# Softmax row sums in a four-layer fp32 kernel: fewer partial sums, two residual buffers, pinned order

## The chip, the cores and the metric

The kernel runs on one core of one Trainium2 chip. The metric is the time of one execution on the device in microseconds (us), taken as the median of several runs. Five engines work side by side, each through its own queue of instructions: TensorE (PE, matmuls; PEld is its weight load), VectorE (DVE), ScalarE (ACT), GpSimd (POOL) and SyncE (SP). DMAs are started from the queues of SP, ACT and POOL.

## The reference

Four layers, each added to its own normalised input, over a tensor of 4 x 384 x 64 x 64 in fp32. Only the first layer is touched:

```python
x_attn = x[:, :PD]            # PD = 96 of 384 channels
x_skip = x[:, PD:]
...
q = qkv[:, :QK].reshape(B, QK, N)          # QK = 16, N = 4096
k = qkv[:, QK:2 * QK].reshape(B, QK, N)
v = qkv[:, 2 * QK:].reshape(B, VD, N)
attn = jax.nn.softmax(jnp.einsum('bcn,bcm->bnm', q, k) * scale, axis=-1)
out = jnp.einsum('bcn,bmn->bcm', v, attn).reshape(B, VD, H, W)
xm = jax.nn.relu(jnp.concatenate([out, x_skip], axis=1))
y = jnp.einsum('oc,bchw->bohw', w_proj, xm)
...
x = x + _L0_conv_ref(_gn(x), ...)
```

So each batch needs a 4096 x 4096 softmax attention over 96 value channels, a ReLU, a 384 x 384 projection and the residual sum. Layers 1 to 3 (a local Fourier filter, a gated convolution block, a dynamic 7 x 7 convolution) follow.

## The kernel before

`attention` (L819) runs for batches b = 0 to 3. A batch is eight **blocks** i of 512 queries, and a block is eight **steps** c of 512 keys. One step does this:

- `scores` (L825): four matmuls, one for each group of 32 rows of the array, write the score tile `sc_s` (four PSUM banks, one buffer). ScalarE turns it into two tiles `probs` of 128 x 1024 by `Exp` (L842): `lo` (tag p0, two buffers) and `hi` (tag p1, three buffers). The scores of step c+1 are traced before the products of step c.
- `products` (L850): twelve matmuls of 32 columns, four side by side, add the step into two PSUM banks `av`. Their order on TensorE is fixed by `together` and `issue_after` (L623, L868).
- `add_up` (L871): the softmax denominators. VectorE adds every `lo` into `acc_lo` (L878; none in step 0). GpSimd starts a DMA which copies (steps 0 and 1, L884) or adds (steps 2 to 6, L886) `hi` into one of two accumulators `acc_hi`, even steps into one and odd ones into the other. The last `hi` is used as it is.

At the end of a block `evacuate` (L888) empties `av`: ScalarE copies two pieces of 32 rows to `av_t` (L893, L895), VectorE one piece of 96 rows to `xm` (L894) and one of 32 to `av_t` (L896). `invert` (L899) sums the four partial tiles (last `hi`, odd, `acc_lo`, even) over their partitions with a matmul of ones, 32 matmuls of 128 columns into `sum_m`, and VectorE takes the reciprocal (L919). In step 1 of the next block `finish` (L922) spreads it (`rd_m`, L926), adds the two halves of the block (L933) and applies ReLU and the scale (L934).

`layer0_end` (L962) then loads the residual block `x_res` (L966, 768 KB over SP's queue, pool `blk`, tag xr, one buffer), makes the 288 other rows of `xm` by ReLU on ScalarE (L967, L971), projects (L978), adds into `x_res` (L985), takes statistics (L649) and stores it with a DMA of GpSimd (L988).

Beside batch b runs `others` (L587): statistics and q, k, v of batch b+1 (L687, L701 to L761) and, from b = 1 on, layer 1 of batch b-1 (L1060 to L1177), spread over the 64 steps by `side_by_side` (L600). A scheduler puts each engine's instructions in order from the traced order, priorities and expected times; an engine runs its list strictly in that order. `keep_in_program_order`, which only the new code uses, queues an instruction behind the one traced just before it on the same engine.

After the attention, `late_block` (L1181) gives layer 2 its input blocks: by turns from the pool `blk` and from a pool `late` opened for it (L574). The branch with `maxima` (L777) is inside an `If` which these data don't take.

Of the kernel before, what the change touches and what calls it, by code (L numbers as in the profile page):

```python
# [29 lines left out]
NJ = 3  # L30
# [252 lines left out]
class _Builder:  # L283
# [222 lines left out]
    def phase_a(self, strips):  # L506
# [3 lines left out]
        with ExitStack() as ctx:  # L510
            self.open_psum(ctx, 2)
            self.ln_exp()
            cp = ctx.enter_context(tc.tile_pool(name="a_const", bufs=1))
            pool = lambda name, bufs: ctx.enter_context(tc.tile_pool(name=name, bufs=bufs))
            self.blk = pool("a_blk", 4)
            self.work = pool("a_work", 2)
            attention = ctx.enter_context(ExitStack())
            self.big = attention.enter_context(tc.tile_pool(name="a_big", bufs=1, side="right"))
            self.probs = attention.enter_context(tc.tile_pool(name="a_probs", bufs=2, side="right"))
            for k in ("r0", "m0", "n0"):  # L520
                setattr(self, k, cp.tile([P, NJ, B], F32, tag=k, name=k))
# [12 lines left out]
            self.first_norm(self.x0_st)  # L534
            self.score_shifts(cp)
            self.ln_exp()
            self.w_proj = self.weight(cp, "w_proj_t")
            self.w_in = self.weight(cp, "w_in_t")
            self.w_out = self.weight(cp, "w_out_t")
            q, k4, vt = self.qkv_tiles()  # L540
            for _ in self.qkv(0, q, k4, vt, self.x0):
                pass
            for _ in self.x_norm(0, self.x0_st):
                pass
            w = lambda tag, name: self.work.tile([P, C], F32, tag=tag, name=name)
            pick, fft = w("tt", "pick")[0:40, 0:P], w("cf", "fft")[0:40]
            lo, hi = _CONST_COLS["pick"]
            nc.sync.dma_start(pick, self.ins["consts"][0:40, lo:hi])
            nc.scalar.dma_start(fft, self.ins["fft_t"])
            pf = self.pm("filter_p")  # L550
            nc.tensor.matmul(pf[:, 0:C], lhsT=pick, rhs=fft, start=True, stop=True)
            self.filt = cp.tile([P, C], F32, tag="filt", name="filt")
            nc.vector.tensor_copy(self.filt, pf[:, 0:C])

            a, c = self.bn_scale_shift(
                "bn2", self.vec("bn2_m"), self.vec("bn2_v"), self.vec("bn2_g"), self.vec("bn2_b")
            )
            self.bn2_c = cp.tile([P, NJ], F32, tag="bn2_c", name="bn2_c")
            nc.vector.tensor_copy(self.bn2_c, c)
            m = self.pm("bn2_rows")  # L560
            t = w("tt", "bn2_a").rearrange("p (j n) -> p j n", j=NJ)
            nc.vector.tensor_copy(t, a.unsqueeze(2).to_broadcast([P, NJ, P]))
            for j in range(NJ):
                nc.tensor.matmul(m[:, j * P : (j + 1) * P], lhsT=t[:, j], rhs=self.ident, start=True, stop=True)
            for j in range(NJ):
                nc.vector.tensor_mul(self.w_proj[:, j], self.w_proj[:, j], m[:, 0:C])
            for b in range(B):
                nxt = self.qkv_tiles() if b + 1 < B else None
                self.side_by_side(b, self.attention(b, q, k4, vt), self.others(b, nxt))
                if nxt is not None:  # L570
                    q, k4, vt = nxt

            attention.close()
            self.late = pool("a_late", 1)  # L574
            self.open_strips(strips)
            layer1, done = self.layer1(B - 1), iter(())
            self.last_x1, ahead, left = [None] * 8, [], 4 * (B - 1)
            for n, _ in enumerate(layer1):
                if n == 20:
                    done = self.strips_of(0, range(B - 1))  # L580
                if next(done, True) is None:
                    left -= 1
                elif not left and len(ahead) < 2 and self.last_x1[3 * len(ahead) + 2] is not None:
                    ahead.append(self.ahead_strips(len(ahead)))
            self.last_strips(ahead)
# [43 lines left out]
                last = job()  # L629
        return last  # L630

    def acc_lo(self, name):
        return self.probs.tile([P, 1024], F32, tag="acc_lo", name=name, bufs=1)

    def acc_hi(self, name):
        return self.probs.tile([P, 1024], F32, tag="acc_hi", name=name, bufs=2)

    def norm_of_stats(self, st):
        mv = self.sm([P, NJ, 2], "gn_mv")
# [137 lines left out]
    def maxima(self, b):  # L777
        nc = self.nc
        for _ in self.x_norm(b):
            pass  # L780
        k = [self.probs.tile([P, 1024], F32, tag=f"p{h}", name="mx_k", bufs=2 + h) for _ in range(2) for h in range(2)]
        q = [self.acc_lo("mx_q"), *(self.acc_hi("mx_q") for _ in range(2))]
        q.append(self.probs.tile([P, 1024], F32, tag="p1", name="mx_q", bufs=3))
        q = [t[:, v * 512 : v * 512 + 512] for t in q for v in range(2)]
        for i in range(8):
            xa = self.layer_norm(self.centered(b, i))
            m = self.pm("mx_q_m")
# [31 lines left out]
    def attention(self, b, q, k4, vt):  # L819
# [3 lines left out]
        tc, nc = self.tc, self.nc  # L823

        def scores(i, c):  # L825
            p = [self.probs.tile([P, 1024], F32, tag=f"p{h}", name="probs", bufs=2 + h) for h in range(2)]
            s = self.p4("sc_s")

            with tc.high_priority(3000) if b else nullcontext():
# [41 lines left out]
        def add_up(c, p):  # L871

            lo, hi = p
            if c == 0:
                self.sums = [self.acc_lo("acc_lo")]
                self.lo_first = lo
            else:
                nc.vector.tensor_add(self.sums[0], self.lo_first, lo)  # L878
                self.lo_first = self.sums[0]
            if c == 7:  # L880
                self.sums.append(hi)
            elif c < 2:
                self.sums.append(self.acc_hi("acc_hi"))
                nc.gpsimd.dma_start(self.sums[1 + c], hi)  # L884
            else:
                nc.gpsimd.dma_start(self.sums[1 + c % 2], hi, accum_op=ALU.add)  # L886

        def evacuate(av):  # L888

            xm = self.work.tile([P, NJ, 512], F32, tag="xm", name="xm", bufs=1)  # L890
            t = self.wk("av_t", "rd", 1)
            with tc.high_priority():
                nc.scalar.copy(t[0:32], av[0][96:128])  # L893
                nc.vector.tensor_copy(xm[0:PD, 0], av[0][0:PD])  # L894
                nc.scalar.copy(t[32:64], av[1][0:32])  # L895
                nc.vector.tensor_copy(t[64:96], av[1][32:64])  # L896
            return xm, t

        def invert(sums):  # L899

            m = self.pm("sum_m")
            lo, even, odd, last = sums
            parts = [t[:, v * 512 : v * 512 + 512] for t in (last, odd, lo, even) for v in range(2)]
            jobs = (
                partial(
                    nc.tensor.matmul,
# [15 lines left out]
        def finish(xm, t, rd):  # L922

            m = self.pm("rd_m")
            for g in range(4):
# [4 lines left out]
                    start=True,  # L930
                    stop=True,
                )
            nc.vector.tensor_add(t[0:PD], t[0:PD], xm[0:PD, 0])  # L933
            nc.vector.scalar_tensor_tensor(xm[0:PD, 0], t[0:PD], 0.0, m[0:PD], ALU.max, ALU.mult)  # L934
            return xm

        self.last_av = None
# [4 lines left out]
        for n_step, (i, c) in enumerate(steps):  # L942
# [7 lines left out]
            if c == 7:  # L950
                evacuated = *evacuate(av), invert(self.sums)
            next(end, None)
            if c == 1 and done is not None:
                end = self.layer0_end(b, i - 1, finish(*done), st)
            if c == 7:
                done = evacuated
            yield
# [4 lines left out]
    def layer0_end(self, b, i, xm, st):  # L962

        nc = self.nc
        blk = slice(i * 512, (i + 1) * 512)
        x = self.block("x_res", self.ins["x"][b], i, "xr", 1)  # L966
        nc.scalar.activation(  # L967
            xm[PD:P, 0], x[PD:P, 0], AF.Relu, bias=self.n0[PD:P, 0, b : b + 1], scale=self.r0[PD:P, 0, b : b + 1]
        )
# [208 lines left out]
        if b == B - 1:  # L1178
            self.last_x1[h] = x

    def late_block(self, n):  # L1181
        return (self.late if n % 2 else self.blk).tile([P, NJ, 512], F32, tag="xr", name="in_x1", bufs=1)

    def ahead_strips(self, n):

        x = self.late_block(n)
        self.nc.gpsimd.dma_start(x, self.x1[B - 1][:, 0, n * 1536 : n * 1536 + 1536].rearrange("p (j n) -> p j n", j=NJ))
        return x

# [185 lines left out]
    def strips_of(self, j, batches):  # L1375

        for b in batches:
            for q in range(4):
                x = self.late_block(b * 4 + q)
                self.strips5(j, b, x.rearrange("p j n -> p (j n)")[:, 0:1024], q * 8, self.pa)  # L1380
                yield

# [984 lines left out]
```

## Time and profile before

| what | us |
|---|---|
| median of 3 runs | 4717.23 (4715.02 to 4718.2) |
| the profiled execution, and its span | 4721.59, 4719.6 |
| TensorE busy in the span | 4310.8 (91%) |
| VectorE, ScalarE, GpSimd busy | 2914.9, 2012.4, 983.4 |

The stages, by stretches of the span (busy us of each engine in the stretch):

| stretch | what runs | PE | DVE | ACT |
|---|---|---|---|---|
| 110 to 560 | attention of batch 0, with q, k, v of batch 1 | 399.1 of 450 | 203.6 | 178.9 |
| 560 to 1130 | batch 1, with layer 1 of batch 0 | 533.1 of 570 | 375.5 | 247.9 |
| 1130 to 1690 | batch 2, with layer 1 of batch 1 | 522.5 of 560 | 363.8 | 247.5 |
| 1690 to 2240 | batch 3, with layer 1 of batch 2 | 501.7 of 550 | 341.2 | 221.4 |
| 2240 to 4720 | layer 1 of batch 3, layers 2 and 3 | 2283.1 of 2480 | 1561.6 | 1073.5 |

To read it: a stretch in which TensorE is busy for nearly all of the time is bound by it, and what is left is the sum of its waits. A fp32 matmul shows as two instructions (twice the count of the code). Durations of matmuls are modelled and overlap, so lengths are best taken from start to start.

### The profile page before, as it was taken

The page shows a single profiled execution, that of the slowest core. Times are in us where ns is not written, and L with a number is a line of the kernel's source. Part 1 is how long each engine was busy: PE and PEld are TensorE (multiplying, and loading weights), DVE is VectorE, ACT ScalarE, POOL GpSimd, SP SyncE. Part 2 cuts the span into 40 slices and gives each one's busy share as a digit, 9 for nine tenths or more (in the row PEclk, how much of TensorE's full clock was granted, in tenths as well). Part 3 has the DMA queues.
Part 4 walks back from the last instruction along what each step waited for, and adds up shares of the span by engine and source line. Part 5 has one row for each costly group of instructions (what it writes and reads, how often), then busy time and mean ns, then how long its engine had stood idle before and what let it go on. Part 6 is the DMA issues. An engine that isn't in the chain of part 4 may idle for free. (4 is left out here: it accounts for less than half of the span.)

```text
span 4719.6 us, 60890 instructions
## 1 busy us (share of the span) xinstructions
PE 4310.8 (91%) x23693; PEld 2332.9 (49%) x23693; DVE 2914.9 (62%) x4800; ACT 2012.4 (43%) x2961; POOL 983.4 (21%) x1007
## 2 busy tenths in 40 slices
PE   6899899999999999997998899699999999898998
PEld 2233333334333333332546888644444444498988
DVE  6533576665666756666687788755541112777898
ACT  4344344344444444443644666521114333664342
POOL 1111111110111110110004566300000000145765
PEclk9999999999999999998999999899999999998999
DMA  5644534343344433443325999976666333897897
GB/s 169 163 116 100 145 94 123 105 122 93 103 111 113 118 101 105 112 114 98 112 99 167 333 326 334 313 261 251 249 233 243 123 132 115 302 337 257 249 310 239
DMA packets 316622, 848.52 MB, mean 180 GB/s; under 512 B 25915, under 2 KB 126374, under 8 KB 305062
## 3 DMA queue, kind: packets, MB, share of 16 engines
q1 hardware_dynamic: 213096, 407.56, 27.3%
q0 software_dynamic: 71136, 291.41, 21.3%
q10 hardware_dynamic: 32094, 145.57, 7.8%
q8 instruction: 190, 3.11, 0.3%
q14 instruction: 106, 0.87, 0.1%
HBM read 433.13 MB, written 293.86 MB: 154 GB/s over the span
## 5 line engine op out<-in xcount | busy, mean ns | idle before, releaser
L629 PE MATMUL av<-probs,vt 128*32 128x512 f32 x5632 | 733.7, 611 | 0.0
L842 ACT ACTIVATE probs<-sc_s 128x1024 f32<-128x1024 f32 x512 | 498.5, 1020 | 520.6 <-PE av L629 322.8
L1147 DVE SCALAR_TENSOR_TENSOR acc<-band,vecs,acc 128x512 f32<-128x512 f32 x708 | 498.9, 746 | 45.1 <-POOL band L1106 34.4
L1437 PE MATMUL conv_m<-toep,z 128*128 128x192 f32 (+1 forms) x2304 | 447.4, 352 | 22.3 <-DVE z L1366 12.3
L1804 PE MATMUL h_m<-f_h,cm_w_t 128*128 128x512 f32 x1008 | 436.1, 595 | 7.4 <-ACT f_h L1741 7.4
L1437 PEld LDWEIGHTS conv_m<-toep,z 128*128 128x128 f32 x2304 | 403.1, 195 | 46.4 <-ACT d_o L1448 13.9
L2199 PE MATMUL conv_m<-toep,z 128*128 128x128 f32 x3072 | 377.6, 280 | 22.1 <-DVE toep L2186 9.4
L878 DVE TENSOR_TENSOR acc_lo<-acc_lo,probs 128x1024 f32<-128x1024 f32 x192 | 234.2, 1220 | 232.4 <-ACT probs L842 232.0
L2199 PEld LDWEIGHTS conv_m<-toep,z 128*128 128x128 f32 x3072 | 363.8, 196 | 25.1 <-issue 8.7
L626 PE MATMUL sc_s<-q,k 32*128 32x512 f32 x512 | 297.6, 662 | 76.5 <-ACT probs L842 76.5
L1683 PE MATMUL h_s<-e_tok,cm_w_t 128*128 128x512 f32 x768 | 362.8, 595 | 4.1 <-DVE e_tok L1668 4.1
L629 PEld LDWEIGHTS av<-probs,vt 128*32 128x32 f32 x5632 | 175.6, 112 | 324.8 <-issue 317.6
L886 POOL DMA_DIRECT2D acc_hi<-probs x160 | 137.2, 857 | 909.7 <-ACT probs L842 833.2
L1418 POOL TENSOR_TENSOR toep<-w,band 128x1280 f32<-128x1280 f32 x96 | 278.3, 2899 | 199.3 <-PE conv_m L1437 187.5
L1804 PEld LDWEIGHTS h_m<-f_h,cm_w_t 128*128 128x128 f32 x1008 | 192.5, 191 | 250.6 <-issue 239.7
L629 PE MATMUL sc_s<-q,k 32*128 32x512 f32 x1536 | 301.1, 662 | 0.0
L1068 PE MATMUL t_m<-w_in_t,xb 128*128 128x384 f32 x768 | 292.6, 513 | 6.5 <-DVE coef L1085 4.8
L626 PE MATMUL av<-probs,vt 128*32 128x512 f32 x512 | 281.1, 632 | 10.5 <-DVE av_t L896 7.2
L978 PE MATMUL proj_m<-xm,w_proj_t 128*128 128x512 f32 x576 | 275.3, 614 | 6.8 <-DVE x_res L985 3.7
L1690 ACT COPY e_h<-h_s 128x1024 f32<-128x1024 f32 x96 | 97.2, 1012 | 400.3 <-PE h_s L1683 400.3
L1692 DVE BATCH_NORM_STATS2 h_st<-e_h 128x6 f32<-128x512 f32 x192 | 123.5, 685 | 217.5 <-ACT e_h L1690 217.5
L1683 PEld LDWEIGHTS h_s<-e_tok,cm_w_t 128*128 128x128 f32 x768 | 146.5, 191 | 188.3 <-issue 183.6
(468 smaller groups left out, 6908.4 us busy)
## 6 DMA issues: line engine op xcount, KB each, us to landing
acc_hi<-probs POOLq DMA_DIRECT2D x224, 512.0 KB, 4.5
d<-d_o ACTq DMA_DIRECT2D x48, 1024.0 KB
c_d<-d SPq DMA_DIRECT2D x48, 1024.0 KB
hid<-e_h ACTq DMA_DIRECT2D x16, 3072.0 KB
f_h<-hid SPq DMA_DIRECT2D x14, 3072.0 KB
x_in<-in_x SPq DMA_DIRECT2D x96, 256.0 KB
x_res<-in_x SPq DMA_DIRECT2D x32, 768.0 KB
xa<-x_res POOLq DMA_DIRECT2D x32, 768.0 KB, 3.9
```

The lines of the kernel that those rows point to most:

```text
L626: first = first()
L629: last = job()
L842: nc.scalar.activation(p[h], s[:, 2 * h : 2 * h + 2].rearrange("p a b -> p (a b)"), AF.Exp, scale=0.25,)
L878: nc.vector.tensor_add(self.sums[0], self.lo_first, lo)
L978: nc.tensor.matmul(m, lhsT=self.w_proj[:, j, o * P : (o + 1) * P], rhs=xm[:, j], start=j == 0, stop=j == NJ - 1,)
L1068: nc.tensor.matmul(m[:, 0:C], lhsT=xb[:, j], rhs=self.w_in[:, j, :], start=j == 0, stop=j == NJ - 1,)
L1147: nc.vector.scalar_tensor_tensor(out, src(j, k), w, done, ALU.mult, ALU.add)
L1418: eng.tensor_tensor(t, self.w53[:, at : at + 160].rearrange("p (m n) -> p m n", n=8).unsqueeze(2).to_broadcast([P, 20, 8, 8]), band.rearra ...
L1437: nc.tensor.matmul(m[:, c * 256 + to : c * 256 + to + 64 * (k1 - k0)], lhsT=self.z_[:, at : at + P], rhs=t[:, 10 * c + k0 : 10 * c + k1].r ...
L1683: nc.tensor.matmul(s[:, v, :], lhsT=w1[:, j, o * P : (o + 1) * P], rhs=t[j][:, v * 512 : (v + 1) * 512], start=j == 0, stop=j == NJ - 1,)
L1804: nc.tensor.matmul(m, lhsT=w2[:, o, j * P : (j + 1) * P], rhs=h[o][:, v * 512 : (v + 1) * 512], start=o == 0, stop=o == 5,)
L2199: nc.tensor.matmul(m[:, ch % 4 * P : (ch % 4 + 1) * P], lhsT=self.z_[:, at : at + P], rhs=t[:, 8 * c + 2 * i : 8 * c + 2 * i + 2].rearrang ...
```

## The change

1. The `hi` of steps 0 to 6 go into one accumulator `acc_hi` instead of two; `hi` has two buffers instead of three. A block of batches 1 to 3 then sums three partial tiles (last `hi`, `acc_lo`, `acc_hi`).
2. In batch 0 there are no accumulating DMAs: VectorE adds `lo` and `hi` of all steps into `acc_lo`, and one partial tile is summed.
3. These additions and DMAs, and the two VectorE operations of `finish`, are pinned in traced order.
4. `evacuate` is ordered VectorE first: the copy of 96 rows, then an addition of the 32 rows of the second bank into `xm` in place of their copy, then the two copies of ScalarE, which go to 64 rows of `av_t`; `finish` adds 64 rows.
5. `finish` is traced in step 0 of the next block instead of step 1; `layer0_end` stays in step 1.
6. `x_res` has two buffers; the pool `late` goes, and layer 2 takes its blocks from the two buffers.

```diff
-            self.late = pool("a_late", 1)
...
-            p = [self.probs.tile([P, 1024], F32, tag=f"p{h}", name="probs", bufs=2 + h) for h in range(2)]
+            p = [self.probs.tile([P, 1024], F32, tag=f"p{h}", name="probs", bufs=2) for h in range(2)]
...
             lo, hi = p
+            add = lambda *of: tc.keep_in_program_order(nc.vector.tensor_add(acc, *of))
             if c == 0:
-                self.sums = [self.acc_lo("acc_lo")]
-                self.lo_first = lo
+                acc, self.first = self.acc("acc_lo"), lo
+                self.sums = [acc]
+            acc = self.sums[0]
+            if b == 0:
+                if c == 0:
+                    add(lo, hi)
+                else:
+                    add(acc, lo)
+                    add(acc, hi)
+                return
+            if c:
+                add(self.first, lo)
+                self.first = acc
+            if c == 7:
+                self.sums.insert(0, hi)
+            elif c == 0:
+                self.sums.append(self.acc("acc_hi"))
+                tc.keep_in_program_order(nc.gpsimd.dma_start(self.sums[1], hi))
             else:
-                nc.vector.tensor_add(self.sums[0], self.lo_first, lo)
-                self.lo_first = self.sums[0]
-            if c == 7:
-                self.sums.append(hi)
-            elif c < 2:
-                self.sums.append(self.acc_hi("acc_hi"))
-                nc.gpsimd.dma_start(self.sums[1 + c], hi)
-            else:
-                nc.gpsimd.dma_start(self.sums[1 + c % 2], hi, accum_op=ALU.add)
+                tc.keep_in_program_order(nc.gpsimd.dma_start(self.sums[1], hi, accum_op=ALU.add))
...
             with tc.high_priority():
+                nc.vector.tensor_copy(xm[0:PD, 0], av[0][0:PD])
+                nc.vector.tensor_add(xm[64:96, 0], xm[64:96, 0], av[1][32:64])
                 nc.scalar.copy(t[0:32], av[0][96:128])
-                nc.vector.tensor_copy(xm[0:PD, 0], av[0][0:PD])
                 nc.scalar.copy(t[32:64], av[1][0:32])
-                nc.vector.tensor_copy(t[64:96], av[1][32:64])
...
-            lo, even, odd, last = sums
-            parts = [t[:, v * 512 : v * 512 + 512] for t in (last, odd, lo, even) for v in range(2)]
+            parts = [t[:, v * 512 : v * 512 + 512] for t in sums for v in range(2)]
...
-            nc.vector.tensor_add(t[0:PD], t[0:PD], xm[0:PD, 0])
-            nc.vector.scalar_tensor_tensor(xm[0:PD, 0], t[0:PD], 0.0, m[0:PD], ALU.max, ALU.mult)
+            pin = tc.keep_in_program_order
+            pin(nc.vector.tensor_add(xm[0:64, 0], xm[0:64, 0], t[0:64]))
+            pin(nc.vector.scalar_tensor_tensor(xm[0:PD, 0], xm[0:PD, 0], 0.0, m[0:PD], ALU.max, ALU.mult))
...
+            if c == 0 and done is not None:
+                xm = finish(*done)
             if c == 1 and done is not None:
-                end = self.layer0_end(b, i - 1, finish(*done), st)
+                end = self.layer0_end(b, i - 1, xm, st)
...
-        x = self.block("x_res", self.ins["x"][b], i, "xr", 1)
+        x = self.block("x_res", self.ins["x"][b], i, "xr", 2)
...
-    def late_block(self, n):
-        return (self.late if n % 2 else self.blk).tile([P, NJ, 512], F32, tag="xr", name="in_x1", bufs=1)
+    def late_block(self):
+        return self.blk.tile([P, NJ, 512], F32, tag="xr", name="in_x1", bufs=2)
```

More of the change, by code (lines that the diff above doesn't have):

```diff
@@ L630, in together, with acc @@
         return last
[L632 to L636, printed above, removed]
+    def acc(self, name):
+        return self.probs.tile([P, 1024], F32, tag=name, name=name, bufs=1)
     def norm_of_stats(self, st):
@@ L780, in maxima @@
             pass
-        k = [self.probs.tile([P, 1024], F32, tag=f"p{h}", name="mx_k", bufs=2 + h) for _ in range(2) for h in range(2)]
-        q = [self.acc_lo("mx_q"), *(self.acc_hi("mx_q") for _ in range(2))]
-        q.append(self.probs.tile([P, 1024], F32, tag="p1", name="mx_q", bufs=3))
+        k = [self.probs.tile([P, 1024], F32, tag=f"p{h}", name="mx_k", bufs=2) for _ in range(2) for h in range(2)]
+        q = [self.acc("acc_lo"), self.acc("acc_hi")]
         q = [t[:, v * 512 : v * 512 + 512] for t in q for v in range(2)]
+        vt = self.big.tile([P, 32, PD], F32, tag="vt", name="mx_q", bufs=2).rearrange("p a n -> p (a n)")
+        q += [vt[:, v * 512 : v * 512 + 512] for v in range(4)]
         for i in range(8):
@@ L1179, in band_out @@
             self.last_x1[h] = x
-    def late_block(self, n):
-        return (self.late if n % 2 else self.blk).tile([P, NJ, 512], F32, tag="xr", name="in_x1", bufs=1)
+    def late_block(self):
+        return self.blk.tile([P, NJ, 512], F32, tag="xr", name="in_x1", bufs=2)
     def ahead_strips(self, n):
-        x = self.late_block(n)
+        x = self.late_block()
         self.nc.gpsimd.dma_start(x, self.x1[B - 1][:, 0, n * 1536 : n * 1536 + 1536].rearrange("p (j n) -> p j n", j=NJ))
@@ L1378, in strips_of @@
             for q in range(4):
-                x = self.late_block(b * 4 + q)
+                x = self.late_block()
                 self.strips5(j, b, x.rearrange("p j n -> p (j n)")[:, 0:1024], q * 8, self.pa)
```

## The prediction

> **What bounds the kernel.** First the page, the table of engines and the windows of four stretches (columns: stretch, length, busy us of PE, PEld, DVE, ACT, POOL with instruction counts, mean granted clock, DMA share, GB/s).
>
> ```profile
> PE 4310.8 (91%) x23693; PEld 2332.9 (49%) x23693; DVE 2914.9 (62%) x4800; ACT 2012.4 (43%) x2961; POOL 983.4 (21%) x1007
> ...
> 110.00:560.00 450.00, 399.06 (x2919) 137.68 (x2923) 203.61 (x326) 178.87 (x220) 53.89 (x73) 0.93 0.50 132
> 560.00:1130.00 570.00, 533.13 (x3444) 206.35 (x3436) 375.47 (x618) 247.92 (x325) 68.64 (x104) 0.99 0.42 112
> ```
>
> TensorE bounds it, and from 110 to 2240 (attention) it idles for 174 us in all: 51 of the 450 in batch 0, some 123 in the rest. A change can save this idle time, matmuls, or badly clocked matmuls. From 2240 on (layer 1 of batch 3, layers 2 and 3) the instruction lists of the two kernels agree on PE, DVE and POOL, so I count nothing there.
>
> Next the waits of PE, 110 to 2240 (engine, what waits, releaser: us in total, times, longest), and those of ACT and of SP's DMA queue:
>
> ```profile
> PE sc_s L626 <- ACT probs L842: 76.5, 44, 5.1
> ...
> ACT xm L967 <- DMA x_res<-in_x: 116.7, 29, 11.5
> ```
>
> The largest wait of PE is a score tile not yet emptied by Exp. Why ACT is late shows in the timeline of ACT and PE around one block boundary of batch 0 (start, us, engine, line, operation, idle before and releaser):
>
> ```profile
> 239.99 0.81 ACT L967 ACTIVATE xm<-x_res,n,r 32x512 f32<-32x512 f32 x1 [4.24 <-DMA x_res<-in_x]
> 240.81 1.52 ACT L971 ACTIVATE xm<-x_res,n,r 128x512 f32<-128x512 f32 x2
> 242.35 1.94 ACT L842 ACTIVATE probs<-sc_s 128x1024 f32<-128x1024 f32 x2
> 244.31 0.57 ACT L895 COPY av_t<-av 32x512 f32<-32x512 f32 x1
> ```
>
> ```profile
> 239.44 0.62 PE L629 MATMUL sum_m<-acc_hi,ones 128*32 128x128 f32 x16
> 239.88 0.62 PE L629 MATMUL sum_m<-acc_lo,ones 128*32 128x128 f32 x16
> 240.31 0.62 PE L629 MATMUL sum_m<-acc_hi,ones 128*32 128x128 f32 x16
> 244.34 0.69 PE L626 MATMUL sc_s<-q,k 32*128 32x512 f32 x1 [3.41 <-ACT probs L842]
> ...
> 246.24 3.89 PE L629 MATMUL av<-probs,vt 128*32 128x512 f32 x19
> ...
> 251.60 2.32 PE L629 MATMUL av<-probs,vt 128*32 128x512 f32 x19
> ```
>
> The skip-channel ReLU (L967) waits for its residual block, the next block's first Exp stands behind it, and PE waits for that Exp. The block comes late because its only buffer must first be stored. After the stall the same products take longer.
>
> **What the Trainium skill says.** "TensorE: Matmul & The Clock Gate", Part 1 (the HAM clock gate): after an idle window of some 3.4 us the array runs at half rate, until it has been active about as long. The trace agrees: after the 3.41 us wait the group of products runs 245.66 to 250.07, 4.41 us; the next, 251.14 to 253.85, 2.71. "Perfetto Trace Analysis", on the engines: ACT, DVE and GpSimd are strict first-in first-out; the Exp behind L967 shows it. "PSUM — Partial Sum Buffer", on bank collisions: ScalarE and VectorE may not touch the same bank and quadrant at once. [...] DVE's copy (L896) waits 87.7 us over 17 boundaries for ACT's (L895). On two buffers for a load no page bears more than the trace.
>
> **The change, part by part.** All against the profiled execution, 4721.6 us (span 4719.6 and 2.0 around it). The median of the runs is 4717.2, 4.4 lower; I take the sum off the median.
>
> *Sums.* From start to start a partial tile costs PE 0.44 us (239.44, 239.88, 240.31). Batch 0 drops three in each of 8 blocks: 24 x 0.44 = 10.5. Batches 1 to 3 drop one in each of 24: 10.5. PE is at its bound, so 21 us go for good.
>
> *x_res.* The list of SP's DMAs has the same order. With two buffers each slot loads a block earlier, against a landing that now comes 4.6 to 5.2 us after issue. So the L967 wait (116.7 us of ACT) goes. Of it PE feels: in the seven boundaries of batch 0, waits of sc_s for probs of 2.32, 3.41, 2.98, 3.44, 5.08, 2.38 and 4.71 = 24.3 us. In batches 1 to 3 fourteen such waits of 1.4 to 4.8 us follow an L967 held by the DMA within 3 to 8 us: 35.0 of the 49.5 us there. Late next would be the Exp by PE's own scores, as in the other steps. 24.3 + 35.0.
>
> *Clock.* Each stall of 3 us or more is followed by 1.7 us lost in one group of products (4.41 less 2.71) and less in the scores around it. About 1.4 x 7 = 10 us for batch 0, 8 for the others: an estimate; bounds 0 and 35.
>
> *Batch 0 on VectorE.* 7 additions a block become 15, 64 more in all. The row of L878 gives the price (192 times, 1220 ns):
>
> ```profile
> L878 DVE TENSOR_TENSOR acc_lo<-acc_lo,probs 128x1024 f32<-128x1024 f32 x192 | 234.2, 1220 | 232.4 <-ACT probs L842 232.0
> ```
>
> 64 x 1.22 = 78 us more on a DVE that is busy 204 of 450; about 63%. A step of PE is 3.65 us (scores 1.07, products 2.6), a pair of additions 2.44, so they lie beside PE: 0. If that cover fails, because statistics of batch 1 (they wait for x_in) stand between the pinned additions, each such delay beyond about a step is felt; bounds 0 and 15. The 56 accumulating DMAs of batch 0, 512 KB each, vanish; I count no gain.
>
> *Evacuation.* Before, the two engines' first pieces ran side by side. Now ACT's copies wait for two DVE operations, with the reciprocal between them: 0.69 + 0.69 + 0.95 (reciprocal) + 0.58, about 3.0 us with gaps. Queued behind ACT's copies are the next Exps, behind PE's first products of the block all of PE. Cover in batch 0 is the sum (now 0.44) and one score group (1.07), 1.5 us; so 1.5 x 7 = 10.5 us of new waits. In batches 1 to 3 layer-1 matmuls give 3 to 7 us of cover: 0. Bounds together 0 and 25.
>
> *finish and the pins, batches 1 to 3.* The addition of step 1 now stands on DVE behind finish (which waits for rd_m, after the first products) and behind layer 1's operations traced before it. It frees `lo` for a later Exp, and that Exp frees the scores. Laying the new list on the timeline of before, step 1's addition ends 14 to 16 us after the sum, Exp of step 2 then ends at 16 to 18, and PE wants the scores at about 16: 0 to 2 us late. I take 0.75 x 24 = 18 us lost. Bounds: 0, and 2 x 24 = 48. In return `coef` is earlier on DVE, and some of the 13.3 us that back_m waits for it may go; not counted.
>
> *One chain of DMAs, two `hi`.* Each addition waits for the previous one: 4.5 us from issue to landing (median of the page's DMA table, 224 times) against steps of 8.5 us or more in batches 1 to 3; a `hi` must be read before the Exp two steps on. Both hidden; if a landing took two steps, ACT and then PE would wait.
>
> *Opening of batch 0 (30 to 191 us).* The first pinned addition comes behind more statistics and weight scaling: PE can do two steps before it needs a buffer back, against five. On the other side fewer DMAs run there. 0; bounds -10 and +10.
>
> Sum: batch 0, 24.3 + 10.5 + 10 - 10.5 = 34; batches 1 to 3, 35.0 + 10.5 + 8 - 18 = 36. Together 70 us: 4721.6 goes to about 4652, and the median to 4647.
>
> **The rivals.** (A) *Given back.* The stalls at boundaries are replaced by the chain of the evacuation and by late additions; only the sums' 21 us and a few more are kept: about -25, 4692. For it: at each boundary several things come ready within 2 us, so removing one shows the next. Against: the wait on the load is the longest of them, and ACT then has slack.
>
> (B) *Slower: the pin gates each block's start.* The mechanism is the step-1 addition behind finish and layer 1's operations, in each of the 24 blocks of batches 1 to 3. Without it the gain is 70 + 18 = 88 us, so it decides from 88 / 24 = 3.7 us a block. Stalls of that length also bring the half clock. At 4.3 us a block it costs 103, net +15: 4732. For it: DVE is busy 66% there, its list is strict, and finish waits for PE. Against: my laying-out gives a margin of 0 to -2, and layer 1's pieces on PE fill some of the wait.
>
> (C) *More.* The clock comes back in full, the pins cost nothing and the opening gains from less DMA traffic: 88 + 15 to 25, about -108, 4609.
>
> (D) That the second buffer doesn't take effect: the SP queue has other loads which wait for stores (xa), 449 us of waits in 545 to 2240. It would bring these blocks late. Then it is case A. In batch 0 I see none in front of x_res that lasts.
>
> **How the numbers follow.** Likeliest (-45 to -100): 0.46, 4647. A and D (-10 to -45): 0.18. C (beyond -100): 0.14. Between: within 0.2%, which is 9.4 us and about what a measurement of this kernel can tell from no change: 0.05. B: 0.17. So faster 0.78, same 0.05, slower 0.17. The range 4600 to 4722 leaves out perhaps 0.04 below and 0.15 above.
>
> **What would show it.** Right: ACT's L967 no longer waits for x_res; PE's wait of sc_s for probs falls from 76.5 to about 20 us; sum matmuls per block fall from 64 to 16 in batch 0 and 48 after; the blocks of batch 0, now 52.4 us apart (mean of six, 191.2 to 505.4), come 46 to 47 apart; new waits of av for av_t or xm of about 1.5 us at its boundaries. Wrong: scores that wait for a probs tile whose Exp waits for DVE's acc_lo in steps 2 and 3 of batches 1 to 3, for 3 us or more; accumulating DMAs that hold an Exp; additions of batch 0 that run two steps late.

## The result, and the profile after

The changed kernel takes 4702.17 us (median of 9 runs, 4696.68 to 4713.22) against 4717.23 (9 runs): a ratio of 0.9961, 95% interval 0.9944 to 0.9979. It is faster by 15 us, where 70 were forecast. The profiled execution took 4713.22 us with a span of 4711.5, at the upper end of its runs.

The stages show where it differs. The starts of the summing matmuls (`sum_m`) in the timeline of PE mark the blocks; the last column is the changed kernel with every pin taken out, one of the experiments below. A **pin** is `keep_in_program_order`. Line numbers below are those of the kernel that is shown; Exp is L839 after the change.

| mark, us | before | after | no pins |
|---|---|---|---|
| first sum of batch 0 | 118.6 | 137.4 | 114.3 |
| last sum of batch 0 | 505.4 | 469.7 | 446.5 |
| last sum of batch 3 | 2228.3 | 2203.6 | 2131.7 |
| from that to the end of the span | 2491.3 | 2507.9 | 2489.4 |

Batch 0 gained 35.7 us although its first block ends 18.8 us later. Batches 1 to 3 took 1722.9 us before and 1733.9 after: 11 us *longer*, with fewer matmuls. The gain of 36 us that was forecast there is missing, and more. The last stage took 16.6 us more, but from 30 us after the last sum on PE, VectorE, GpSimd and SyncE run the same list in both kernels, and this execution lies 11 us above the median; the other profiled executions of this document take 2484.5 to 2500.6 us there. So this is not read as an effect of the change.

First, the waits of PE, 110 to 2240, of the changed kernel:

```profile
PE sc_s L625 <- ACT probs L839: 48.1, 38, 3.9
...
PE av L625 <- ACT av_t L901: 13.6, 5, 3.0
```

then those of ACT in the same stretch:

```profile
ACT probs L839 <- DVE acc_lo L871: 187.7, 61, 15.0
...
ACT probs L839 <- DMA acc_hi<-probs: 12.3, 6, 3.4
```

The reader is to see an exchange. ACT's wait for `x_res` (116.7 us before) is gone from the list, as forecast. In its place Exp waits 187.7 us for VectorE's additions; from 560 on it is 151.6 us, against 0.4 before. PE's wait for scores fell only from 76.5 to 48.1, and what is left has new causes. Followed back along ACT's queue, of the 48.1 us 28.7 stand behind an Exp that waits for an addition, 9.8 behind ACT's copies of the new evacuation, which wait for VectorE's, and 7.2 behind an Exp that waits for an accumulating DMA. By window (stretch, length, busy PE, PEld, DVE, ACT, POOL, granted clock, DMA share, GB/s):

```profile
110.00:560.00 450.00, 402.76 (x2761) 134.84 (x2750) 286.50 (x409) 189.73 (x233) 20.54 (x29) 0.95 0.27 81
```

VectorE is at 64% in this stretch, where 63% was worked out, and the DMA share fell from 0.50 to 0.27. Batch 0 in steady state is close to all work: its blocks are 45 us apart against 52. This is one of its boundaries, in PE's timeline:

```profile
288.27 0.31 PE L628 MATMUL sum_m<-acc_lo,ones 128*32 128x128 f32 x3
288.39 0.27 PE L625 MATMUL sum_m<-acc_lo,ones 128*32 128x128 f32 x1
288.40 0.50 PE L628 MATMUL sum_m<-acc_lo,ones 128*32 128x128 f32 x11
288.83 0.69 PE L625 MATMUL sc_s<-q,k 32*128 32x512 f32 x1
...
291.31 1.92 PE L628 MATMUL av<-probs,vt 128*32 128x512 f32 x16 [0.34 <-ACT av_t L902]
```

The scores follow the sum at once. The new evacuation leaves a hole of 0.34 us here and at most 0.49 at the other boundaries, not 1.5: eight product instructions of the new block run before the copy of the second bank (L902) has ended, at 291.25 in ACT's timeline.

What goes wrong in the other batches shows first in VectorE's timeline early in batch 1:

```profile
503.96 1.21 DVE L871 TENSOR_TENSOR acc_lo<-acc_lo,probs 128x1024 f32<-128x1024 f32 x1
511.47 1.33 DVE L683 BATCH_NORM_STATS2 x_st<-x_in 128x6 f32<-128x512 f32 x2 [6.31 <-DMA x_in<-in_x]
515.26 0.69 DVE L683 BATCH_NORM_STATS2 x_st<-x_in 128x6 f32<-128x512 f32 x1 [2.46 <-DMA x_in<-in_x]
518.49 0.69 DVE L683 BATCH_NORM_STATS2 x_st<-x_in 128x6 f32<-128x512 f32 x1 [2.54 <-DMA x_in<-in_x]
...
530.43 1.31 DVE L683 BATCH_NORM_STATS2 x_st<-x_in 128x6 f32<-128x512 f32 x2 [4.64 <-DMA x_in<-in_x]
...
533.01 1.22 DVE L871 TENSOR_TENSOR acc_lo<-acc_lo,probs 128x1024 f32<-128x1024 f32 x1
```

and the Exp that this addition held, in ACT's:

```profile
534.32 1.94 ACT L839 ACTIVATE probs<-sc_s 128x1024 f32<-128x1024 f32 x2 [15.03 <-DVE acc_lo L871]
```

Two additions of the softmax stand 29 us apart. Between them VectorE waits for loads of `x_in`, for statistics of the *next* batch that were traced before the addition. A pinned addition may not pass them.

This is the longest single wait, but not the usual one: after batch 0 waits for `x_in` hold Exp only at this turn. Inside the batches the first addition of a block stands behind `finish` (L940) and behind layer 1's sums (`xa_out`, L1182), and both of these wait for TensorE. VectorE in batch 1:

```profile
936.27 0.68 DVE L940 SCALAR_TENSOR_TENSOR xm<-xm,rd_m 96x512 f32<-96x512 f32 x1 [1.87 <-PE rd_m L931]
938.18 0.69 DVE L1182 TENSOR_TENSOR xa_out<-xa_out,out_m 128x512 f32<-128x512 f32 x1 [1.23 <-PE out_m L1179]
938.79 1.22 DVE L871 TENSOR_TENSOR acc_lo<-probs 128x1024 f32<-128x1024 f32 x1
```

and the Exp behind it:

```profile
940.10 1.94 ACT L839 ACTIVATE probs<-sc_s 128x1024 f32<-128x1024 f32 x2 [11.98 <-DVE acc_lo L871]
```

From the last sum of batch 0 to that of batch 3 Exp waits 170.3 us for additions. During these waits VectorE works for 126 us on what is queued, and idles for 52: 19.5 in front of L940, 15.0 in front of L1182 and 10.2 for `x_in`.

### The profile page after: what moved, and what is told of

Read it like the earlier page. It is cut to its first block, busy times and chain, and to the rows that moved or that the text cites. A ratio compares the mean times of both kernels' runs of the same rounds, so it can differ in the third digit from the quotient of the medians.

```text
span 4711.5 us, 59491 instructions
## 1 busy us (share of the span) xinstructions
PE 4310.6 (91%) x22925; PEld 2325.3 (49%) x22925; DVE 2984.0 (63%) x4864; ACT 2015.5 (43%) x2961; POOL 952.8 (20%) x951
## 5 line engine op out<-in xcount | busy, mean ns | idle before, releaser
L839 ACT ACTIVATE probs<-sc_s 128x1024 f32<-128x1024 f32 x512 | 502.0, 1021 | 581.6 <-PE av L628 202.2
L628 PE MATMUL av<-probs,vt 128*32 128x512 f32 x5632 | 729.3, 602 | 2.2 <-ACT av_t L902 2.2
L871 DVE TENSOR_TENSOR acc_lo<-acc_lo,probs 128x1024 f32<-128x1024 f32 x256 | 311.7, 1218 | 7.0 <-ACT probs L839 2.6
L625 PE MATMUL av<-probs,vt 128*32 128x512 f32 x512 | 272.5, 614 | 13.9 <-ACT av_t L901 13.6
L892 POOL DMA_DIRECT2D acc_hi<-probs x144 | 125.9, 874 | 698.6 <-ACT probs L839 328.4
L1691 PEld LDWEIGHTS h_s<-e_tok,cm_w_t 128*128 128x128 f32 x768 | 146.5, 191 | 187.7 <-issue 183.0
```

The costliest lines, as they stand in the source:

```text
L625: first = first()
L839: nc.scalar.activation(p[h], s[:, 2 * h : 2 * h + 2].rearrange("p a b -> p (a b)"), AF.Exp, scale=0.25,)
L871: add = lambda *of: tc.keep_in_program_order(nc.vector.tensor_add(acc, *of))
L1691: nc.tensor.matmul(s[:, v, :], lhsT=w1[:, j, o * P : (o + 1) * P], rhs=t[j][:, v * 512 : (v + 1) * 512], start=j == 0, stop=j == NJ - 1,)
```

## The experiments

Each is compared with the kernel before by the ratio of its runs, and with the other experiments by the marks. Differences between two experiments in us are of medians from different series, in which the kernel before itself gave 4717 to 4732; they are good to some 10 us (experiment 9 lies 10 above experiment 4 at an equal ratio). The marks are of one execution each. How far those can be trusted shows where kernels run the same lists: batches 1 to 3 take 1685.2 and 1694.2 us in experiments 4 and 2, with the same lists there on all engines, and the first sum comes at 114.3 to 120.9 us in experiments 4, 5, 10, 12 and 13, which have VectorE's list of batch 0 in common up to its end. "Unpinned" means the changed kernel without any `keep_in_program_order`.

**1. Two `x_res` buffers, one accumulator and two `hi` in the kernel before.** The lines for the tile sizes and for the pool `late` follow and are not shown.

```diff
-        x = self.block("x_res", self.ins["x"][b], i, "xr", 1)
+        x = self.block("x_res", self.ins["x"][b], i, "xr", 2)
-            elif c < 2:
+            elif c == 0:
                 self.sums.append(self.acc_hi("acc_hi"))
-                nc.gpsimd.dma_start(self.sums[1 + c], hi)
+                nc.gpsimd.dma_start(self.sums[1], hi)
             else:
-                nc.gpsimd.dma_start(self.sums[1 + c % 2], hi, accum_op=ALU.add)
+                nc.gpsimd.dma_start(self.sums[1], hi, accum_op=ALU.add)
```

> The kernel before with two x_res buffers, one acc_hi and two hi, and nothing else of the change (no pins, no VectorE batch 0, old evacuation, finish in step 1). Theory P (the gain of the second x_res buffer in batches 1 to 3 is real, and the pinned additions take it back): batch 0 loses most of its 24 us of waits, batches 1 to 3 some 30 us of theirs and 10 us of sums; total -50 to -65 us, about 4660. Rival N (the stalls of batches 1 to 3 are replaced by something else whenever the load is early, pins or not): batches 1 to 3 gain at most the 10 us of sums; total -25 to -35 us, about 4688.

4634.17 us against 4726.45 in the same series, ratio 0.9807 (0.9770 to 0.9845): 92 us less, better than even theory P. Last sum of batch 0 at 467.2, batches 1 to 3 in 1676.4 us, 46 less than before. PE's waits for scores from 560 on fell from 49.5 to 18.9 us. So the gain in batches 1 to 3 is real, N falls, and something else in the change takes it away. Two of its six parts bring by themselves all that the unpinned change brings (0.9797).

**2. Pins in batch 0 only.**

```diff
-            add = lambda *of: tc.keep_in_program_order(nc.vector.tensor_add(acc, *of))
+            pin = tc.keep_in_program_order if b == 0 else lambda x: x
+            add = lambda *of: pin(nc.vector.tensor_add(acc, *of))
...
-                tc.keep_in_program_order(nc.gpsimd.dma_start(self.sums[1], hi, accum_op=ALU.add))
+                nc.gpsimd.dma_start(self.sums[1], hi, accum_op=ALU.add)
...
-            pin = tc.keep_in_program_order
+            pin = lambda x: x
             pin(nc.vector.tensor_add(xm[0:64, 0], xm[0:64, 0], t[0:64]))
```

> The changed kernel with the pins kept for the additions of batch 0 alone: in batches 1 to 3 additions, accumulating DMAs and finish are placed by the scheduler. Theory P: ACT's waits of Exp for acc_lo in batches 1 to 3 (170 us) fall below 60, and these batches lose 30 to 45 us: about 4665. Rival N: the waits of TensorE for scores stay near 42 us in batches 1 to 3 with another releaser and the time stays within 8 us of 4702.

4651.00 us, 0.9838 (0.9802 to 0.9874). Exp waits 15.0 us for `acc_lo` in the whole of 110 to 2240. Batches 1 to 3 take 1694.2 us in place of 1733.9: 40 less. Theory P holds.

**3. finish in step 1.**

```diff
-            if c == 0 and done is not None:
-                xm = finish(*done)
             if c == 1 and done is not None:
-                end = self.layer0_end(b, i - 1, xm, st)
+                end = self.layer0_end(b, i - 1, finish(*done), st)
```

> The changed kernel with finish traced in step 1, as before, all pins kept. Theory P in the form of the prediction (step 1's addition is late because it stands behind finish): batches 1 to 3 lose 15 to 25 us, about 4682. If it is the pins as such (additions behind layer 1's operations traced before them) and not finish: within 8 us of 4702.

4696.94 us, 0.9938 (0.9918 to 0.9958); batches 1 to 3 in 1729.1 us, 5 less, which is within the spread. That is the second outcome: the pins as such, not the place of finish. Exp still waits 128.8 us for `acc_lo` from 560 on, against 151.6. VectorE no longer idles for finish inside these waits, but 27.5 us in front of layer 1's sums in place of 15.0: the next operation in the queue takes over.

**4. No pins at all.** The pins of experiment 2, taken out in batch 0 too.

> The changed kernel without any pin. Theory P: batches 1 to 3 as in the run with pins in batch 0 alone. Batch 0: if the late first additions (first sum at 137 us against 119) come from the pin, the first sum comes 10 to 19 us earlier here; if they come from VectorE's 15 additions a block as such, it stays at 135 or later. Total about 4655 in the first case, 4670 in the second; Rival N: about 4700.

4628.71 us, 0.9797 (0.9760 to 0.9834): 98 us less than before, and 73 less than with the pins. The first sum comes at 114.3 us in place of 137.4. In batches 1 to 3 the pins cost 48.6 us: 28.0 of it is PE's idle time (134.6 against 106.6), the rest the same matmuls taking longer, at a mean granted clock of 0.967 against 0.983. So in the opening too it is the pin and not the number of additions. In VectorE's timeline of the changed kernel the first addition of the whole attention stands here:

```profile
96.98 1.49 DVE L566 TENSOR_TENSOR w_proj_t<-w_proj_t,bn_rows 128x384 f32<-128x384 f32 x3 [0.94 <-PE bn_rows L564]
98.38 1.22 DVE L871 TENSOR_TENSOR acc_lo<-probs 128x1024 f32<-128x1024 f32 x1
99.52 0.69 DVE L683 BATCH_NORM_STATS2 x_st<-x_in 128x6 f32<-128x512 f32 x1
```

and in that of the kernel without pins here:

```profile
50.87 1.21 DVE L871 TENSOR_TENSOR acc_lo<-probs 128x1024 f32<-128x1024 f32 x1
```

Pinned, it comes 47 us later, behind the scaling of `w_proj`, which was traced before it.

**5. Only the additions of batches 1 to 3 pinned** (in the unpinned kernel).

```diff
-            add = lambda *of: nc.vector.tensor_add(acc, *of)
+            pin = tc.keep_in_program_order if b else lambda x: x
+            add = lambda *of: pin(nc.vector.tensor_add(acc, *of))
```

> The unpinned kernel with one pin put back: the VectorE additions of batches 1 to 3 alone (finish, the accumulating DMAs and batch 0 stay free). If the additions carry the loss of batches 1 to 3 (they queue behind statistics that wait for x_in, and behind layer 1's multiply-adds): Exp waits for acc_lo come back to 120 us or more of ACT, the time goes from 4629 to 4665 to 4680. Rival (the pins of the DMAs or of finish carry it): within 10 us of 4629.

4665.41 us, 0.9883 (0.9859 to 0.9907): 37 more than unpinned. The wait of Exp is back as a line of ACT's waits, 110 to 2240:

```profile
ACT probs L839 <- DVE acc_lo L872: 189.3, 55, 17.7
```

Batches 1 to 3 take 1716.5 us, against 1685.2 unpinned and 1733.9 with all pins. The additions by themselves cost 31, where all pins cost 49.

**6. The old evacuation in the unpinned kernel**, with finish adding 96 rows again.

```diff
+                nc.scalar.copy(t[0:32], av[0][96:128])
                 nc.vector.tensor_copy(xm[0:PD, 0], av[0][0:PD])
-                nc.vector.tensor_add(xm[64:96, 0], xm[64:96, 0], av[1][32:64])
-                nc.scalar.copy(t[0:32], av[0][96:128])
                 nc.scalar.copy(t[32:64], av[1][0:32])
+                nc.vector.tensor_copy(t[64:96], av[1][32:64])
```

> The unpinned kernel with the evacuation of before (ACT first, 96 rows of av_t, no addition on VectorE). Theory of the prediction (the new order leaves a hole of 1.5 us at each boundary of batch 0, nothing in the others): blocks of batch 0 come 43.6 apart in place of 45.1, the time falls by 10 us to about 4618. Rival (the two chains are as long, or ACT's two copies ahead of the next Exps cost as much): within 4 us of 4629.

4609.00 us, 0.9761 (0.9738 to 0.9784): 20 us less by the medians, 17 by the ratios, whose intervals still overlap; 19.0 by the last sum of batch 3, and experiment 11 repeats it. It lies elsewhere than expected: from the first to the last sum batch 0 gains 3.3 us only (332.3 to 329.0), and 17.7 come after it. The new order costs where I had put zero, and little where I had put 10.5. The way it costs shows in the traces: in the unpinned kernel 11.1 us of PE's waits for scores stand behind ACT's copies that wait for VectorE's, and with the old order none do.

**7. One x_res buffer in the unpinned kernel**, and the pool `late` with it.

```diff
-        x = self.block("x_res", self.ins["x"][b], i, "xr", 2)
+        x = self.block("x_res", self.ins["x"][b], i, "xr", 1)
```

> The unpinned kernel with one x_res buffer (and the late pool) as before. Prediction's terms: 24 us of waits and 10 of clock in batch 0, 35 and 8 in batches 1 to 3 come back: about 77 us, 4706; batch 0 blocks 50 to 51 apart. Rival (in batches 1 to 3 the wait on the load was only one of several that end together): 35 to 45 us, about 4670.

4710.95 us, 0.9963 (0.9951 to 0.9975). The second buffer is worth 82 us by the medians and 78 by the ratios, where the terms said 77. The wait returns, in ACT's list, 110 to 2240:

```profile
ACT xm L976 <- DMA x_res<-in_x: 121.6, 30, 11.3
```

Up to the last sum of batch 0 it costs 45.6 us (446.5 to 492.1), and 35.9 in batches 1 to 3. From the second to the last sum of batch 0, where the two kernels do the same in the same blocks, it is 318.3 us against 270.8. Taking PE's time from start to start and leaving out what the trace lists as idle, 31.9 us of these 47.5 are waits, and products and scores take 15.2 us longer for the same instructions (198.8 against 183.6), at a mean granted clock of 0.92 against 1.00. In batches 1 to 3 the waits are 18.6 and the slower products and scores 14.0.

**8. Batch 0 by accumulating DMAs, as the other batches, in the unpinned kernel.**

```diff
-            if b == 0:
-                if c == 0:
-                    add(lo, hi)
-                else:
-                    add(acc, lo)
-                    add(acc, hi)
-                return
```

> The unpinned kernel with batch 0 summed as the other batches (accumulating DMAs for hi, three partial tiles). By the terms of the sum: 8 x 2 x 0.44 = 7 us more matmuls in batch 0, else nothing: 4636. If the accumulating DMAs also slow the opening (they share the DMA engines with the loads): first sum at 120 or later in place of 114, about 4645. If VectorE's 15 additions a block cost PE waits that were overlooked: 4629 or less.

4657.54 us, 0.9866 (0.9842 to 0.9891): 29 more, none of the three cases. The first sum comes at 118.6, which is within its spread, but the second 78.1 us later in place of 61.5, where all kernels here that keep VectorE's sums in batch 0 and no priority need 59.4 to 62.5. So some 17 us are lost in the second block. Which part of this is DMA traffic and which is GpSimd's queue was not separated. The six blocks that follow take 272.3 us against 270.8. The longer sums are 5.2 us of PE there, but the hole behind the evacuation closes (PE idles 1.4 us in place of 3.8): next to the new evacuation little of the shorter sum is left in batch 0.

**9. Only the first block of batch 0 pinned** (in the unpinned kernel; `blocks_done` is set at the end of the first block).

```diff
-            add = lambda *of: nc.vector.tensor_add(acc, *of)
+            pin = tc.keep_in_program_order if b == 0 and not self.blocks_done else lambda x: x
+            add = lambda *of: pin(nc.vector.tensor_add(acc, *of))
```

> The unpinned kernel with the 15 additions of the first block of batch 0 pinned, nothing else. If the opening's loss is the first pinned additions standing behind batch 0's statistics and the scaling of w_proj: first sum at 135 to 138 us in place of 114, the time 4629 + 20 = 4649. If it is the many additions beside batch 1's statistics further on: first sum at 120 or earlier, within 8 us of 4629.

First sum at 139.2 us, and all marks stay some 23 us late up to the last sum of batch 3 (2155.1 against 2131.7). 15 additions reproduce the whole loss of the opening: the four kernels with this block pinned have their first sum at 137.4 to 139.2, so the loss is 17 to 25 us against the spread of the others. The median, 4639.16 (0.9797, 0.9766 to 0.9827), is 10 us above the unpinned kernel's with an equal ratio, so these runs don't settle how much of it reaches the end.

**10, 12 and 13. The other pins:** those of the accumulating DMAs and of finish together, the DMAs' alone, finish's alone, each put back into the unpinned kernel.

```diff
-                nc.gpsimd.dma_start(self.sums[1], hi, accum_op=ALU.add)
+                tc.keep_in_program_order(nc.gpsimd.dma_start(self.sums[1], hi, accum_op=ALU.add))
...
-            pin = lambda x: x
+            pin = tc.keep_in_program_order
             pin(nc.vector.tensor_add(xm[0:64, 0], xm[0:64, 0], t[0:64]))
```

> The changed kernel with its additions free, and the pins of the accumulating DMAs and of finish kept: what is left of the 73 us between the changed kernel (4702) and the unpinned one (4629) after the additions (22 in batch 0, 37 in batches 1 to 3). If these pins cost by themselves: 4629 + 14 = 4643, the loss in batches 1 to 3. If they only cost where the additions are late as well: within 6 us of 4629.

4685.70 us, 0.9899 (0.9871 to 0.9928): neither of the two outcomes, it costs 57 by the medians, and 49.8 in batches 1 to 3.

> The unpinned kernel with the accumulating DMAs pinned in traced order on GpSimd, nothing else. If the DMAs carry the 57 us of the pins of DMAs and finish: Exp's waits for acc_hi's DMA about 30 us as there (6.7 unpinned), time 4670 to 4690. If finish carries them: within 10 us of 4629.

> The unpinned kernel with finish's two VectorE operations pinned in traced order, nothing else. If finish carries the 57 us (the operations of layer 1 that were traced before and after it can no longer pass it while it waits for TensorE): TensorE's waits for coef and x_res grow, time 4665 to 4690. If the DMAs carry them: within 10 us of 4629.

The DMAs' pins alone: 4684.11 us, 0.9902 (0.9873 to 0.9931), 55 more than unpinned; batches 1 to 3 in 1739.6 us. Finish's alone: 4632.93, 0.9804 (0.9780 to 0.9829), 1684.1 us. The DMAs carry it, finish nothing. A part of the reason shows on POOL's queue around the start of batch 1 with the DMAs pinned:

```profile
469.64 0.71 POOL L996 DMA_DIRECT2D xa<-x_res  x1 [26.00 <-DVE x_res L993]
470.24 0.66 POOL L890 DMA_DIRECT2D acc_hi<-probs  x1
476.90 0.90 POOL L892 DMA_DIRECT2D acc_hi<-probs  x1 [6.01 <-issue]
483.19 0.87 POOL L892 DMA_DIRECT2D acc_hi<-probs  x1 [5.38 <-issue]
...
498.64 0.86 POOL L892 DMA_DIRECT2D acc_hi<-probs  x1 [5.66 <-issue]
```

and without any pin:

```profile
455.61 0.87 POOL L892 DMA_DIRECT2D acc_hi<-probs  x1 [4.83 <-issue]
460.67 0.86 POOL L892 DMA_DIRECT2D acc_hi<-probs  x1 [4.19 <-issue]
472.02 0.75 POOL L996 DMA_DIRECT2D xa<-x_res  x1 [10.50 <-DVE x_res L993]
472.66 1.01 POOL L892 DMA_DIRECT2D acc_hi<-probs  x1
```

The pinned first copy of the batch (L890) stands behind a store that was traced before it and that waits for VectorE. It is issued at 470.24 us; the free one goes ahead of that store, at 445.11, and its batch began 6 us earlier. The pinned ones are then issued one after the other, every 6 to 9 us, and a `hi` comes free late. ACT's list (470 to 2190) agrees:

```profile
ACT probs L839 <- DMA acc_hi<-probs: 39.4, 20, 5.1
```

It was 6.7 unpinned. Batches 1 to 3 lose 54.4 us, of which 32.0 are idle time of PE (138.6 against 106.6); the rest is matmuls that take longer, at a granted clock of 0.965 against 0.983. How these 32.0 us divide between the late `hi` and layer 1's operations, whose order shifts as well, stays open.

**11. Old evacuation, and finish in step 1, unpinned** (edits of 6 and 3).

> The unpinned kernel with the old evacuation and with finish traced in step 1: what is left of the change is two x_res buffers, one accumulator and batch 0 on VectorE. By the run with pins (finish in step 1 moved nothing) within 6 us of 4609. If step 0 helps once nothing is pinned (the additions are then free to go ahead of it): 5 to 10 us slower.

4611.74 us, 0.9746 (0.9717 to 0.9776): with finish in step 0 it was 0.9761, so no difference shows.

**14. Priority in place of a pin** (old evacuation, unpinned).

```diff
-            add = lambda *of: nc.vector.tensor_add(acc, *of)
+            def add(*of):
+                with tc.high_priority():
+                    nc.vector.tensor_add(acc, *of)
```

> The unpinned kernel with the old evacuation and the additions placed by high priority instead of by a pin. If late additions still cost something when the scheduler places them: up to 10 us faster than 4609. If they don't: within 5 us of 4609, or slower, as they then go ahead of work that TensorE wants.

4630.24 us, 0.9790 (0.9759 to 0.9820), 21 slower than without the priority by the medians. Its batch 0 is late (last sum 466.5 against 445.1), while the stretch from there to the last sum of batch 3 takes 1670.0 us against 1667.5. Giving the additions priority gains nothing in batches 1 to 3, so placed freely they are not late there; in batch 0 it delays the first blocks.

## Why the prediction was off

The forecast was 70 us and 15 came. Step by step:

| term, us (positive: gained) | forecast | the runs |
|---|---|---|
| sums (PE start to start: 13.6 to 4.4; 49.0 to 35.7) | 21 | 9.2 + 13.3 = 22.5 |
| second x_res with the clock (7) | 34 + 43 = 77 | 82: 45.6 in batch 0, 35.9 after |
| batch 0 on VectorE, beyond its sums (8) | 0 | 17 by the second block; 29 - 7 = 22 by the medians |
| evacuation (6) | -10.5, in batch 0 | -20, mostly after batch 0 |
| opening, pinned (9, marks) | 0 | -17 to -25 |
| pins in batches 1 to 3 (marks, 4 to all pins) | -18 | -49 |
| all | 70 | 15 |

The terms were measured one at a time, against different kernels. They add up to some 30 to 40, not to 15; in the profiled executions the changed kernel is 24.7 us ahead at the last sum of batch 3. What the difference is made of stays open.

*Right.* The stall at the boundary, its cause and its price, by the trace of before: L967's wait is gone and the batch 0 blocks are 45 us apart, where 46 to 47 were named. Experiment 1 has just these terms, 77 for the buffer and 32 x 0.44 = 14 for the sums, 91 in all. Its medians differ by 92; by the marks batch 0 gained 38, as put, and batches 1 to 3 gained 46, where 54 were put. "TensorE: Matmul & The Clock Gate" of the Trainium skill, Part 1, gives the half rate after an idle window, and the traces agree: from the second to the last sum of batch 0 products and scores took 194.6 us before and 183.9 after, 10.7 less, where 10 were put; the mean granted clock went from 0.95 to 1.00. In the trace of before a stall of 2.98 us, at 294.5, was enough: the products behind it took 4.70 us, in place of 2.71 for the next group.

*Right in sum, wrong in parts.* Batch 0 gained 35.7 us where 34 were forecast, and that is partly luck. The pinned opening cost 17 to 25, and taking the accumulating DMAs out of batch 0 gave about as much. I gave the opening "0; bounds -10 and +10" although I had seen that the first addition would stand behind the scaling of `w_proj`. I never placed it in time: in the trace of before the first addition starts at 58.1 us and the last scaling of `w_proj` at 108.4, so a delay of some 50 us, with two `lo` buffers, could be read there.

*The step that failed.* "I take 0.75 x 24 = 18 us lost" for finish and the pins in batches 1 to 3; 49 were lost. I priced only the addition of step 1, behind finish and layer 1, in the blocks inside a batch. That wait is real (L940 and L1182 in batch 1), and it was not put too low: of the 28 us that PE idles more with the pins, 11 lie inside the batches. The other 17 lie at the three turns from one batch to the next, 13 of them at the first. The sum left the turns out, although a pin binds every addition to everything traced before it on VectorE, and there this is statistics that wait for `x_in`: they are in the 15 us of one Exp, and from the last sum of batch 0 to the first of batch 1 it took 76.4 us before, 88.6 after, 72.8 without pins. And the 18 us counted waits alone; some 20 of the 49 are slower matmuls. Naming finish was no help either: when it moves, layer 1's sums take its place (experiment 3), and its own pin costs nothing (13). The recorded bound of 48 is what came.

*The step that was left out.* "One chain of DMAs ... Both hidden" counts the landing of a DMA and not its place in GpSimd's queue. Pinned there, behind stores that wait, the DMAs cost 54 us in batches 1 to 3 by themselves. This doesn't come on top of the additions' 31: with all pins these batches lose 49. That the same Exps are then held by whichever is later would explain it, but was not shown.

*The evacuation.* Its hole in batch 0 was put at 1.5 us a boundary and is 0.5 at most; where layer 1 was to cover it, at "0", ACT's copies hold the next Exp (11.1 us of PE's waits in the unpinned kernel). The rule on bank collisions that the prediction names does not explain these waits: L895 copies rows 0 to 32 of the second bank and L896 rows 32 to 64, two different quadrants. The traces show that the copies wait for one another, and not why.

*The rivals.* Case A (4692) came nearest, and its reason "removing one shows the next" is what the waits of ACT look like. But in experiment 1 PE's waits for scores fall from 76.5 to 25.8 us and stay there: most of the next was made by the pins. B named the pin as the danger; its mechanism, step 1 behind finish and layer 1, is there, but only as a part of the loss. Batches 1 to 3 by themselves did get slower, by 11 us, as B had it. D falls: the wait for `x_res` is gone. C asked for pins that cost nothing and for an opening that gains from less DMA traffic; without pins its 4609 is missed by 20 us. The kernel of experiment 6 has that time, but it has another evacuation, so this is no proof of C.

The version of experiment 6, the change without its pins and with the old evacuation, beats both kernels: 4609.00 us, a ratio of 0.9761 to the kernel before, which is some 113 us of its 4717.

## What to carry to other kernels

Before pinning an instruction in traced order, list what was traced ahead of it on that queue and ask of each what it waits for: a pin makes all these waits its own, and a DMA issue has such a queue too. Do this at the turn of a stage as well as in its middle. A stall on PE has to be priced with the slow matmuls behind it, here about half as much again. Edits that help can hide one that costs, so when a change with six parts moves the time little, take each out alone.

## What the runs showed of the hardware that I had not expected

With one `x_res` buffer PE stalled once a block, for 3.6 to 7.1 us. Between the second and the last sum of batch 0 this made 31.9 us more of waits, and the same products and scores took 198.8 us in place of 183.6: the slower matmuls behind the stalls added half of what the stalls themselves cost.
